# Two graph layers on one core: logits of both array halves one unit ahead, and the order of sums, values and projections at the end of attention

## The chip, the core and the metric

The kernel runs on one core of a Trainium2 chip. The metric is device time in microseconds (us), the median of three runs. One execution was also profiled; where a text speaks of a moment ("763.26") it is microseconds from the start of that execution's span. Engines are named as the profile names them: PE is TensorE's matmuls and PEld its weight loads, DVE is VectorE, ACT ScalarE, POOL GpSimd, SP SyncE. L503 is line 503 of the kernel.

## The reference

`x` is (8, 2048, 256) in float32, `adj` a (2048, 2048) matrix of 0 and 1. Two layers, each with a residual. Layer 0 is attention with 4 heads of 64, masked by `adj`; the softmax is taken separately in each of 8 chunks of 256 keys, and the chunks' contexts are summed. Layer 1 is a graph attention with one head.

```python
h = relu(layernorm(x))
q, k, v = heads(h @ Wq.T + bq), heads(h @ Wk.T + bk), heads(h @ Wv.T + bv)
scores = clip(einsum('bhnd,bhjcd->bhnjc', q, chunks(k)) / 8, -10, 10)
scores = where(mask == 0, -10, scores)
attn = softmax(scores, axis=-1)                    # within one chunk j
ctx = einsum('bhnjc,bhjcd->bhnd', attn, chunks(v)) # sums over chunks too
x = x + layernorm(ctx @ Wo.T + bo + h) * gamma + beta

h = relu(layernorm(x)) @ W
e = leaky_relu((h @ a1)[:, :, None] + (h @ a2)[:, None, :], 0.01)
x = x + relu(softmax(where(adj == 0, -1e9, e)) @ h)
```

(The `h` that is added before the layernorm of layer 0 is the layer's normalised input.)

## The kernel before

The 8 batches run one after the other. Attention of a batch is cut into 32 steps: 4 blocks of 512 queries by 8 chunks of 256 keys. Behind it layer 1 of the batch runs in 16 pieces (`products`, L994), and near its end the next batch's attention starts.

**Tiles of the array.** Heads are 64 wide, so attention uses the 128 x 128 array in tiles of 64 rows by 32 columns: four column tiles side by side, and two halves by rows. Half 0 holds rows 0 to 63, half 1 rows 64 to 127. Both halves can run at once, each on its own data. In a step there is:

- `logits` (L503), four units `o` = 0 to 3. `ORDER = [(0, 1), (0, 0), (1, 1), (1, 0)]` gives the head pair `p` and the half `i` of each, so units 0 and 2 run in half 1 and units 1 and 3 in half 0. A unit fills a PSUM tile `ps_s` of two banks; there are two such tiles.
- `clip` (L543, DVE) takes a unit out of PSUM into `e`, applying the bounds and the mask; `exponentials` (L552, ACT) works in place; `add` (L558, POOL) adds the two 128-key tiles of a head pair into `both`, of which there are two buffers, one per head pair of a step.
- `values` (L519): 32 matmuls. The context lies in two banks `ps_n`, one for each half `c` of the head columns. The "first values" are those with (half, c) = (0, 1) and (1, 0); the "later values" are the other pairing and add to the same banks, now from the other half.
- `sums` (L531): the denominators, 4 matmuls with ones in half 1 and 4 in half 0, into one bank `ps_t`.
- `invert` (L563 and L564, ACT: logarithm and exponential of its negative), `scale` (L573, DVE, two per step), which frees the `ps_n` banks, and `gather` (L578, POOL), which adds the product to the context by a DMA.

A float32 matmul shows as two records in the trace, so a group of one half's logits of a unit is x16, and of both halves x32.

**Fences.** Two halves that write one bank must not run together. `fence(before, after)` (L475) issues a SyncE nop that waits for the matmuls of `before`, and the matmuls of `after` wait for the nop. SyncE also issues many of the DMAs, in the same queue: among them, at the end of attention, the fetches of `hT` for layer 1 (`low.fetch1`) and for the next batch (`ahead.fetch(1)`), and in batch 0 also the stores of `ahead.send(3)`.

**Order.** All engines follow the order in which the program emits. Attention is a software pipeline of frames f = 2 to 34, each with `begin(f)` and `end(f)`, and with pieces of other work (output projection, layernorm, the next batch's work) hung in at 2f and 2f + 1. In a plain frame TensorE does, in this order: later values of step f−3; logits 1 (half 0) and 2 (half 1) of step f−1; first values of step f−2; logits 3 of step f−1 in half 0 around the upper sums of step f−2 in half 1; logits 0 of step f in half 1 around the lower sums of step f−2 in half 0. So half 1 is one logit unit ahead of half 0. Step 0 and the first part of step 1 are computed by `early(0)` to `early(3)` inside the last layer-1 pieces of the batch before.

At the end, frame 32 still has logits 3 of step 31 in half 0, with half 1 without work beside it; frame 33 has the projection q of the next batch's first block (L447), first values of step 31, the projection k, and then `last_sums`: sums and later values of step 31 together. Behind this comes the part between the layers: four token tiles of `low.values` (L843), each followed by `low.keep` with a copy on ACT (L851) and the copy `sd` on DVE (L852); `mid.stats1` (L356 and L357); the values projection `ahead.values` (L461); a part of q (L447); and the output projection (L721). The fourth block's output chain (L757 to L792, DVE, ACT and POOL) runs around it. In the last batch there is no next one: layer 1's `zero.values` take the place of q, and weights of layer 1 (L971, L977) that of k.

Of the kernel before, what the change touches and what calls it, by code (L numbers as in the profile page):

```python
# [28 lines left out]
def gnn_two_layers(  # L29
# [26 lines left out]
    TB = NB // P  # L56
    NNB = N // NB
    NCH = N // CHUNK
    KT = CHUNK // P
# [14 lines left out]
    def ps_t():  # L74
        return ps.tile([P, 512], F32, tag="t", name="ps_t")
# [397 lines left out]
    def fence(before, after):  # L473

        nop = nc.sync.nop()  # L475
        for x in before:
            tc.add_manual_dep(nop.ins, x.ins.name, SYNC, reason="both write one bank of PSUM")
        for x in after:
            tc.add_manual_dep(x.ins, nop.ins.name, SYNC, reason="both write one bank of PSUM")


    class Attention:
# [42 lines left out]

        def sums(self, n, half):
            rows = slice(half * DH, (half + 1) * DH)
            if half:
                self.total[n] = ps_t()
            return [  # L530
                nc.tensor.matmul(  # L531
                    self.total[n][h * Q:(h + 1) * Q, :], ones[rows, :], self.both[n, h // 2][rows, h % 2, :],
                    start=half == 1, stop=half == 0,
                )
                for h in range(HEADS)
            ]
# [46 lines left out]
        def early(self, part):  # L583

            if part == 0:
                for kt in range(KT):
                    self.logits(0, 0, kt)
                    self.logits(0, 1, kt)
            elif part == 1:
                for o in range(2):  # L590
                    self.clip(0, o)
                    self.exponentials(0, o)
                for kt in range(KT):
                    self.logits(0, 2, kt)
                    self.logits(0, 3, kt)
            elif part == 2:
                self.clip(0, 2)
                self.exponentials(0, 2)
                self.clip(0, 3)
                self.add(0, 0)  # L600
            if part == 3:
                for kt in range(KT):
                    self.logits(1, 0, kt)

# [3 lines left out]
        def begin(self, f, pieces=()):  # L610

            self.run(pieces, "first")
            if (f - 3, 0) in self.before:
                made = {}
                for kt in range(KT):
                    for half, c in ((0, 0), (1, 1)):
                        made.setdefault(c, []).extend(self.values(f - 3, half, c, kt))
                for c in range(2):
                    fence(self.before.pop((f - 3, c)), made[c])
            if (f - 1, 0) in self.s:  # L620
                self.clip(f - 1, 0)
            if self.has(f - 3):
                self.invert(f - 3)
            if self.has(f - 2):
                self.exponentials(f - 2, 3)
            if self.has(f - 1):
                self.exponentials(f - 1, 0)
            if self.has(f - 3) and not self.has(f - 1):
                self.scale(f - 3, 0)
                self.scale(f - 3, 1)  # L630
            self.run(pieces, "pe")
            if self.has(f - 1):
                for kt in range(KT):
                    self.logits(f - 1, 1, kt)
                    self.logits(f - 1, 2, kt)
                if self.has(f - 3):
                    self.scale(f - 3, 0)
                    self.scale(f - 3, 1)
            if self.has(f - 2):
                self.add(f - 2, 1)  # L640
            if self.has(f - 3):
                self.gather(f - 3)
            self.rest = pieces

        def end(self, f, pieces=()):
            self.run(pieces, "first")
            if self.has(f - 1):
                self.clip(f - 1, 1)
            self.run(pieces, "pe1")
            if self.has(f - 1):  # L650
                self.clip(f - 1, 2)
            self.run(pieces, "after")
            self.run(self.rest, None)
            if self.has(f - 1):
                self.exponentials(f - 1, 1)
                self.exponentials(f - 1, 2)
            if self.has(f - 2):
                made = {}
                for kt in range(KT):
                    for half, c in ((0, 1), (1, 0)):  # L660
                        made.setdefault(c, []).extend(self.values(f - 2, half, c, kt))
                for c in range(2):
                    self.before[f - 2, c] = made[c]
            if self.has(f - 1):
                self.logits(f - 1, 3, 0)
            if self.has(f - 2) and self.has(f - 1):
                sums = self.sums(f - 2, 1)
            if self.has(f - 1):
                self.logits(f - 1, 3, 1)
            if self.has(f):  # L670
                self.logits(f, 0, 0)
            self.run(pieces, None)
            self.run(pieces, "pe")
            if self.has(f - 2) and self.has(f - 1):
                fence(sums, self.sums(f - 2, 0))
            elif self.has(f - 2):
                self.last_sums(f - 2)
            if self.has(f):
                self.logits(f, 0, 1)
            if self.has(f - 1):  # L680
                self.clip(f - 1, 3)
                self.add(f - 1, 0)

        def last_sums(self, n):

            upper = self.sums(n, 1)
            made = {0: self.values(n, 0, 0, 0), 1: self.values(n, 1, 1, 0)}
            made[0] += self.values(n, 0, 0, 1)
            lower = self.sums(n, 0)
            made[1] += self.values(n, 1, 1, 1)  # L690
            for c in range(2):
                fence(self.before.pop((n, c)), made[c])
            fence(upper, lower)

        @staticmethod
        def run(pieces, kind):
# [5 lines left out]
    class Between:  # L702
        def __init__(self, nb, proj, attention, sd, sums):
            self.nb, self.proj, self.attention, self.sd, self.sums = nb, proj, attention, sd, sums
            self.hn0, self.pp, self.hns = {}, {}, []

            self.adder = nc.gpsimd
# [201 lines left out]
    class Layer1:  # L909
        def __init__(self, b, blocks, sd, sums):  # L910
            self.b, self.blocks, self.sd, self.sums = b, blocks, sd, sums
            self.src = {}
            self.cd = small.tile([P, 2, NT], F32, tag="cd", name="cd", bufs=2)
# [253 lines left out]
    for b in range(B):  # L1167
        sd = small.tile([P, 2, NT], F32, tag="sd", name="sd", bufs=2)
        sums = small.tile([P, NNB, FC], F32, tag="sums", name="sums", bufs=2)
        blocks = [Between(nb, projs[b], att, sd, sums) for nb in range(NNB)]  # L1170
        zero, low, mid, last = blocks
# [24 lines left out]
        if b == 0:  # L1196
# [4 lines left out]
            for nb, ns in enumerate(beats):  # L1201
# [3 lines left out]
                n = ns[-1]  # L1205
# [53 lines left out]
            block.adder = nc.vector  # L1259
        if ahead:  # L1260
            for t in range(TB):
                mid.stats1([t])
                low.values(t, ps_h if t < 2 else ps_t)
                low.keep(t)
            low.sum1()
            zero.fetch1()
            mid.power1()
# [60 lines left out]
        else:  # L1328
# [6 lines left out]
            mid.shift1()  # L1335
            accs[0] = one.accumulators(0)
            early(0)
            mid.norm1(0)
            mid.norm1(1)
# [20 lines left out]
            for t2 in range(2):  # L1360
                last.gamma(t2)
                last.add(t2)
            early(1)
            last.stats1(range(TB))
            last.power1()
            last.shift1()
            weights(3)
            last.norm1(0)
            last.norm1(1)
            early(2)  # L1370
            last.ends(0)
            one.total()
# [90 lines left out]
```

## Time and profile before

| | |
|---|---|
| median of 3 runs | 3513.77 us (3513.32 to 3514.57) |
| the profiled execution | 3513.01 us |
| its span | 3511.2 us, granted TensorE clock 1.000 |
| TensorE matmul, weight load | 3498.5 us, 2300.0 us busy |
| VectorE, ScalarE, GpSimd | 2630.4, 1959.2, 1825.5 us busy |
| one step's matmuls for logits, values, sums | 1335.2, 1121.2, 548.7 us busy in all (L503, L519, L531) |
| first values of step 30 to q, second batch | 763.26 to 769.38 |
| q, first values of step 31, k, `last_sums` | from 769.38, 773.01, 774.88, 778.51 |
| first matmul of layer 1's values (L843), second batch | 781.25 |

Busy times of a row in the profile add up what overlaps only once, so that a TensorE row with one half at work counts as one with both. A row of a timeline joins like instructions that follow each other: start, time from the first start to the last end, engine, line, operation, tile, and how many; in brackets the idle time before it and what ended it.

### The profile page before, as it was taken

The page shows a single profiled execution, that of the slowest core. Times are in us where ns is not written, and L with a number is a line of the kernel's source. Part 1 is how long each engine was busy: PE and PEld are TensorE (multiplying, and loading weights), DVE is VectorE, ACT ScalarE, POOL GpSimd, SP SyncE. Part 2 cuts the span into 40 slices and gives each one's busy share as a digit, 9 for nine tenths or more (in the row PEclk, how much of TensorE's full clock was granted, in tenths as well). Part 3 has the DMA queues.
Part 4 walks back from the last instruction along what each step waited for, and adds up shares of the span by engine and source line. Part 5 has one row for each costly group of instructions (what it writes and reads, how often), then busy time and mean ns, then how long its engine had stood idle before and what let it go on. Part 6 is the DMA issues. An engine that isn't in the chain of part 4 may idle for free.

```text
span 3511.2 us, 104599 instructions
## 1 busy us (share of the span) xinstructions
PE 3498.5 (100%) x46076; PEld 2300.0 (66%) x46076; DVE 2630.4 (75%) x3983; ACT 1959.2 (56%) x2961; POOL 1825.5 (52%) x1198
## 2 busy tenths in 40 slices
PE   9999999999999999999999999999999999999999
PEld 5455775667765577566876758656686655864568
DVE  7887677877678676786767867678686785857876
ACT  6777426763267633676336763367623776147751
POOL 5687017870278702786037850378503784047841
PEclk9999999999999999999999999999999999999999
DMA  7545323443234431444324443244432335224331
GB/s 246 129 108 123 94 87 73 97 113 102 68 87 86 118 100 61 92 93 109 102 61 92 92 105 102 66 91 87 119 105 64 79 85 125 63 55 92 80 78 53
DMA packets 171320, 332.13 MB, mean 95 GB/s; under 512 B 28656, under 2 KB 90352, under 8 KB 170864
## 3 DMA queue, kind: packets, MB, share of 16 engines
q1 hardware_dynamic: 129712, 205.36, 18.6%
q0 software_dynamic: 32832, 119.03, 18.5%
q8 instruction: 360, 5.90, 0.7%
q10 hardware_dynamic: 8320, 1.05, 0.2%
q14 instruction: 96, 0.79, 0.1%
HBM read 156.50 MB, written 51.44 MB: 59 GB/s over the span
## 4 chain that ended last, share of the span: by engine, by line
PE 97%; DVE 1%; ACT 1%; POOL 1%; issue 0%; DMA 0%; ACTq 0%; DVEq 0%; POOLq 0%
PE ps_s L503 25%; PE ps_n L519 25%; PE ps_s L994 12%; PE ps_t L531 6%; PE ps_n L994 6%; PE ps_t L994 6%; PE ps_t L743 2%; PE ps_t L447 2%; PE ps_n L447 2%; PE ps_s L447 2%; PE ps_t L461 2%; PE ps_n L461 1%; PE ps_n L843 1%; PE ps_t L843 1%; PE ps_z L296 0%
## 5 line engine op out<-in xcount | busy, mean ns | idle before, releaser
L543 DVE SCALAR_TENSOR_TENSOR e<-ps_s,bound 128x1024 f32<-128x1024 f32 x1024 | 1219.3, 1221 | 401.3 <-PE ps_s L503 396.4
L558 POOL TENSOR_TENSOR both<-e 128x1024 f32<-128x1024 f32 x512 | 1222.4, 2418 | 541.8 <-PE ps_t L531 244.6
L503 PE MATMUL ps_s<-q,k 64*32 64x512 f32 x16384 | 1335.2, 590 | 0.1
L552 ACT ACTIVATE e<-e 128x1024 f32<-128x1024 f32 x1024 | 1049.3, 1049 | 456.2 <-DVE e L543 438.8
L519 PE MATMUL ps_n<-e,v 64*32 64x512 f32 x16384 | 1121.2, 589 | 0.0
L503 PEld LDWEIGHTS ps_s<-q,k 64*32 64x32 f32 x16384 | 505.2, 106 | 403.3 <-issue 277.9
L519 PEld LDWEIGHTS ps_n<-e,v 64*32 64x32 f32 x16384 | 522.0, 107 | 366.3 <-issue 266.5
L531 PE MATMUL ps_t<-both,ones 64*32 64x512 f32 x4096 | 548.7, 590 | 0.0
L994 PE MATMUL ps_s<-g,w 128*128 128x257 f32 x2048 | 448.5, 380 | 0.0
L994 PEld LDWEIGHTS ps_s<-g,w 128*128 128x128 f32 x2048 | 388.4, 190 | 56.0
L573 DVE TENSOR_TENSOR prod<-ps_n,rz 128x512 f32<-128x512 f32 x448 | 288.7, 687 | 135.0 <-ACT rz L564 86.5
L1017 POOL TENSOR_TENSOR x<-x,r 128x256 f32<-128x256 f32 x124 | 90.7, 745 | 457.8 <-ACT r L1015 457.0
L977 DVE SCALAR_TENSOR_TENSOR w<-bound,w 128x1024 f32<-128x1024 int8 x256 | 314.7, 1229 | 8.7
L367 POOL TENSOR_TENSOR krn<-krn,mv 128x4 f32<-128x4 f32 x28 | 6.8, 243 | 566.1 <-DVE w L971 566.1
L994 PE MATMUL ps_n<-g,w 128*128 128x257 f32 x1024 | 292.4, 382 | 0.0
L994 PE MATMUL ps_t<-g,w 128*128 128x257 f32 x1024 | 289.7, 380 | 0.0
L563 ACT ACTIVATE rz<-ps_t 128x512 f32<-128x512 f32 x256 | 152.6, 596 | 237.3 <-PE ps_t L531 164.2
L971 DVE TENSOR_SCALAR w<-src,cd 128x512 f32<-128x512 f32 x512 | 263.2, 556 | 18.1 <-ACT src L951 14.2
L994 PEld LDWEIGHTS ps_n<-g,w 128*128 128x128 f32 x1024 | 192.8, 190 | 44.3 <-issue 17.6
L578 POOL DMA_DIRECT2D ctxT<-prod x224 | 192.3, 858 | 56.5 <-DVE prod L573 49.5
L531 PEld LDWEIGHTS ps_t<-both,ones 64*32 64x32 f32 x4096 | 152.3, 105 | 100.7 <-SPq L475 45.1
L994 PEld LDWEIGHTS ps_t<-g,w 128*128 128x128 f32 x1024 | 193.8, 189 | 28.2
(139 smaller groups left out, 2975.2 us busy)
## 6 DMA issues: line engine op xcount, KB each, us to landing
ctxT<-prod POOLq DMA_DIRECT2D x224, 512.0 KB, 5.0
bound<-bound_d SPq DMA_DIRECT2D x125, 512.0 KB, 4.7
turned_d<-squares SPq DMA_DIRECT2D x232, 128.0 KB, 2.9
hT<-turned_d SPq DMA_DIRECT2D x58, 512.0 KB, 4.5
rows<-in_adj_dram SPq DMA_DIRECT2D x32, 512.0 KB, 5.3
x<-in_x_dram SPq DMA_DIRECT2D x32, 512.0 KB, 6.3
out_dram<-x SPq DMA_DIRECT2D x31, 512.0 KB, 2.6
xp<-in_x_dram SPq DMA_DIRECT2D x28, 512.0 KB, 4.4
```

The lines of the kernel that those rows point to most:

```text
L447: nc.tensor.matmul(in_key_order(pp) if i == 0 else pp, w[:, di, do * P:(do + 1) * P], h, start=di == 0, stop=di == FC - 1,)
L503: nc.tensor.matmul(self.s[n, o][c * Q:(c + 1) * Q, kt, :], self.k[p][rows, at:at + Q], self.q[p][rows, nb * NB:(nb + 1) * NB], start=True, ...
L519: made.append(nc.tensor.matmul(self.num[n, c][h * Q:(h + 1) * Q, :], self.v[rows, j * KT + kt, at:at + Q], self.e[n, p][rows, i * KT + kt, :],
L531: nc.tensor.matmul(self.total[n][h * Q:(h + 1) * Q, :], ones[rows, :], self.both[n, h // 2][rows, h % 2, :], start=half == 1, stop=half == 0,)
L543: nc.vector.scalar_tensor_tensor(self.e[n, p][:, i * KT:(i + 1) * KT, :], self.s.pop((n, o)), -CLIP * SC, bounds[nb, j // 4][:, j % 4 * KT ...
L552: nc.scalar.activation(e, e, AF.Exp, scale=1.0 / SC)
L558: nc.gpsimd.tensor_tensor(self.both[n, p], e[:, 0], e[:, 1], op=ALU.add)
L573: nc.vector.tensor_tensor(dst[:, c, :], self.num.pop((n, c)), self.rz[n], op=ALU.mult)
L578: nc.gpsimd.dma_start(self.ctxT[nb], self.prod.pop(n), accum_op=ALU.add)
L971: nc.vector.tensor_scalar(w[:, i, :], self.src[nb], self.cd[:, 0, j:j + 1], self.cd[:, 1, j:j + 1], op0=ALU.mult, op1=ALU.max,)
L977: nc.vector.scalar_tensor_tensor(two, bounds1[nb, j // 8][:, j % 8 - 1:j % 8 + 1, :], 0.0, two, op0=ALU.is_gt, op1=ALU.mult)
L994: nc.tensor.matmul(accs[t][:, 0:F + 1], w[:, i, t * P:(t + 1) * P], g[:, j, :], start=j == 0, stop=j == NT - 1,)
```

## The change

Logit unit 1 of the next step moves ahead: in `end(f)` logits 1 and 0 of step f now stand where logits 3 of step f−1 and 0 of step f stood, and in `begin(f)` units 3 and 2 of step f−1 go together. Clips and exponentials follow their units. Later values are emitted with half 1 first. `early(3)` computes units 1 and 0 of step 1 together. Frame 32 has no logits left: it has first values of step 30, lower sums, later values of the same step, upper sums. In frame 33 the upper sums of step 31 come directly behind q, then first values and lower sums; the inversion is emitted ahead of k, and later values come behind k. `sums` no longer depends on which half is first. Between the layers, the values of a token tile and their copies are emitted ahead of the statistics of the tile before.

```diff
         def sums(self, n, half):
             rows = slice(half * DH, (half + 1) * DH)
-            if half:
+            first = n not in self.total
+            if first:
                 self.total[n] = ps_t()
...
-                    start=half == 1, stop=half == 0,
+                    start=first, stop=not first,
...
             if part == 3:
                 for kt in range(KT):
+                    self.logits(1, 1, kt)
                     self.logits(1, 0, kt)
+                self.clip(1, 1)
...
         def begin(self, f, pieces=()):
...
             if (f - 3, 0) in self.before:
-                made = {}
-                for kt in range(KT):
-                    for half, c in ((0, 0), (1, 1)):
-                        made.setdefault(c, []).extend(self.values(f - 3, half, c, kt))
-                for c in range(2):
-                    fence(self.before.pop((f - 3, c)), made[c])
+                self.later_values(f - 3)
             if (f - 1, 0) in self.s:
                 self.clip(f - 1, 0)
-            if self.has(f - 3):
+            if (f - 3) in self.total:
                 self.invert(f - 3)
-            if self.has(f - 2):
-                self.exponentials(f - 2, 3)
             if self.has(f - 1):
+                self.exponentials(f - 1, 1)
                 self.exponentials(f - 1, 0)
-            if self.has(f - 3) and not self.has(f - 1):
+            if self.has(f - 3) and not self.has(f):
                 self.scale(f - 3, 0)
                 self.scale(f - 3, 1)
             self.run(pieces, "pe")
             if self.has(f - 1):
                 for kt in range(KT):
-                    self.logits(f - 1, 1, kt)
+                    self.logits(f - 1, 3, kt)
                     self.logits(f - 1, 2, kt)
-                if self.has(f - 3):
+                if self.has(f) and self.has(f - 3):
                     self.scale(f - 3, 0)
                     self.scale(f - 3, 1)
...
         def end(self, f, pieces=()):
...
-                self.clip(f - 1, 1)
+                self.clip(f - 1, 3)
...
-                self.exponentials(f - 1, 1)
+                self.exponentials(f - 1, 3)
                 self.exponentials(f - 1, 2)
...
-                self.logits(f - 1, 3, 0)
...
-                sums = self.sums(f - 2, 1)
...
-                self.logits(f - 1, 3, 1)
...
+            if self.has(f):
+                self.first_values(f - 2)
+                self.logits(f, 1, 0)
+                sums = self.sums(f - 2, 1)
+                self.logits(f, 1, 1)
+                self.logits(f, 0, 0)
+                self.run(pieces, None)
+                self.run(pieces, "pe")
+                fence(sums, self.sums(f - 2, 0))
+                self.logits(f, 0, 1)
+                self.clip(f, 1)
+            elif self.has(f - 1):
+                self.first_values(f - 2)
+                sums = self.sums(f - 2, 0)
+                self.later_values(f - 2)
+                fence(sums, self.sums(f - 2, 1))
+                self.run(pieces, None)
+                self.run(pieces, "pe")
+            elif self.has(f - 2):
+                sums = self.sums(f - 2, 1)
+                self.first_values(f - 2)
+                fence(sums, self.sums(f - 2, 0))
+                self.run(pieces, None)
+                self.invert(f - 2)
+                self.run(pieces, "pe")
+                self.later_values(f - 2)
...
-        def last_sums(self, n):
...
+        def later_values(self, n):
+            made = {0: [], 1: []}
+            for kt in range(KT):
+                for half, c in ((1, 1), (0, 0)):
+                    made[c] += self.values(n, half, c, kt)
             for c in range(2):
                 fence(self.before.pop((n, c)), made[c])
...
             for t in range(TB):
-                mid.stats1([t])
                 low.values(t, ps_h if t < 2 else ps_t)
                 low.keep(t)
+                if t:
+                    mid.stats1([t - 1])
+            mid.stats1([TB - 1])
```

In the changed kernel the lines from `sums` on lie one lower (sums L532, clip L544, add L559, scale L574), `fence` stays at L475, and those between the layers lie five lower (L848, L857).

More of the change, by code (lines that the diff above doesn't have):

```diff
@@ L599, in early @@
                 self.clip(0, 3)
+                self.exponentials(0, 3)
                 self.add(0, 0)
@@ L654, in end @@
             if self.has(f - 1):
-                self.exponentials(f - 1, 1)
+                self.exponentials(f - 1, 3)
                 self.exponentials(f - 1, 2)
[L657 to L663, printed above, removed]
-            if self.has(f - 1):
-                self.logits(f - 1, 3, 0)
@@ L666, in end @@
-            if self.has(f - 2) and self.has(f - 1):
-                sums = self.sums(f - 2, 1)
-            if self.has(f - 1):
-                self.logits(f - 1, 3, 1)
[L670 to L679, printed above, removed]
@@ L680, in end @@
-            if self.has(f - 1):
-                self.clip(f - 1, 3)
-                self.add(f - 1, 0)
-        def last_sums(self, n):
[L686 to L690, printed above, removed]
+            if self.has(f):
[24 more added lines that the diff above has]
+                self.later_values(f - 2)
@@ new lines, in end, with first_values @@
+            if self.has(f - 1):
+                self.add(f - 1, 0)
+        def first_values(self, n):
+            made = {0: [], 1: []}
+            for kt in range(KT):
+                for half, c in ((0, 1), (1, 0)):
+                    made[c] += self.values(n, half, c, kt)
+            for c in range(2):
+                self.before[n, c] = made[c]
+        def later_values(self, n):
+            made = {0: [], 1: []}
+            for kt in range(KT):
+                for half, c in ((1, 1), (0, 0)):
+                    made[c] += self.values(n, half, c, kt)
@@ L691, in last_sums @@
             for c in range(2):
                 fence(self.before.pop((n, c)), made[c])
-            fence(upper, lower)
         @staticmethod
```

## The prediction

> **What bounds the kernel now.** I read the page first (engine rows, clock, chain that ended last), then TensorE's timeline inside a batch and across the place where attention of a batch ends and layer 1 begins (I call it the joint), then GpSimd's and VectorE's timelines there, and the list of waits.
>
> ```profile
> PE 3498.5 (100%) x46076; PEld 2300.0 (66%) x46076; DVE 2630.4 (75%) x3983; ACT 1959.2 (56%) x2961; POOL 1825.5 (52%) x1198
> PE 97%; DVE 1%; ACT 1%; POOL 1%; issue 0%; DMA 0%; ACTq 0%; DVEq 0%; POOLq 0%
> ```
>
> PE is busy all the time at granted clock 1.00 and 97% of the chain is its own. Busy does not mean full, though: the array is cut into two halves of 64 rows, and a row of this trace is as busy with one half running as with both. So PE's time has to be counted in passes. A plain frame:
>
> ```profile
> 606.14 2.00 PE L519 MATMUL ps_n<-e,v 64*32 64x512 f32 x32
> 607.86 2.00 PE L503 MATMUL ps_s<-q,k 64*32 64x512 f32 x32
> 609.58 2.00 PE L519 MATMUL ps_n<-e,v 64*32 64x512 f32 x32
> 613.87 2.00 PE L519 MATMUL ps_n<-e,v 64*32 64x512 f32 x32
> ```
>
> x32 with both halves takes 607.86−606.14 = 1.72 us, which is 4 passes of 0.43 (0.429). From one later-values group to the same one a frame on, 613.87−606.14 = 7.73 = 18 passes, and 18 is what each half has to do (8 logits, 8 values, 2 sums). Plain frames are full. Here the Trainium skill ("Trainium Kernel Development and Optimization", section "Best Practices") has a rule: judge the distance to the roofline by the share of weight loads, not of matmuls. Row: PEld 66%. By the rule a third, 0.34 × 3511 = 1190 us, would be open; by the pass count, nothing inside a frame. I take the pass count, so gains can come only from where a half stands idle. Those places:
>
> ```profile
> 925.38 1.95 PE L503 MATMUL ps_s<-q,k 64*32 64x512 f32 x32
> 943.41 1.92 PE L503 MATMUL ps_s<-q,k 64*32 64x512 f32 x16
> 945.26 0.92 PE L994 MATMUL ps_n<-g,w 128*128 128x257 f32 x3
> 763.26 2.23 PE L519 MATMUL ps_n<-e,v 64*32 64x512 f32 x32
> 769.38 3.70 PE L447 MATMUL ps_s<-hT,wqT 128*128 128x512 f32 x8
> 773.01 1.95 PE L519 MATMUL ps_n<-e,v 64*32 64x512 f32 x32
> 774.88 3.70 PE L447 MATMUL ps_s<-hT,wkT 128*128 128x512 f32 x8
> 781.25 2.01 PE L843 MATMUL ps_s<-w1s,hT 128*128 128x258 f32 x8
> 784.84 1.89 PE L461 MATMUL ps_n<-wvT,hT 128*128 128x256 f32 x8
> 787.28 1.99 PE L461 MATMUL ps_t<-wvT,hT 128*128 128x256 f32 x8 [0.55 <-DVE sd L852]
> ```
>
> At 943.41 a lone x16 takes 1.85 us, as long as an x32 (1.88). From the first values of step 30 (763.26) to q (769.38) are 6.12 us = 14 passes, of which half 1 needs 10.
>
> **The change, part by part** (clock of the second batch).
>
> *Early units and frame 32.* Logits (1,1) join (1,0) at 943.41: x32 for x16, +0.03. In frame 32 the four passes of logit unit 3 of step 31 are gone from half 0, and later values of step 30 move in from frame 33. What remains after the first values is 6 passes per half. But half 1's later values now stand directly behind half 0's first values in the same PSUM bank, and a fence (a SyncE nop) orders them. Row: `PEld ps_t L531 <- SPq L475`, 45.1 us in 247 waits, 0.18 each, where four passes lie between the parties. Here none do: half 0's last record starts 764.89, lasts 0.59, the nop and the reload bring half 1 to about 765.68 in place of 765.08. The skill's "TensorEngine Tiling (Array Packing)", section "Gotcha 1: PSUM Pressure", speaks against the new order: two row tiles may not use one bank at a time and software must synchronise. Priced by the row this is 0.2, by the two parties back to back 0.6; I take 0.6 (0.4 per batch apart, 3 us in all). Then 6 × 0.429 + 0.11: q at 768.36. Gain 1.02.
>
> *Frame 33, last sums ahead of k.* Sums of step 31 in half 1 now come directly behind q. They need `both` of step 31, two GpSimd adds:
>
> ```profile
> 767.90 4.68 POOL L558 TENSOR_TENSOR both<-e 128x1024 f32<-128x1024 f32 x2 [0.83 <-PE ps_t L531]
> ```
>
> There are two such buffers, so those adds wait for the sums of step 30. These end at 768.43 now (half 1 is last). So: 768.43 + 0.17 + 4.68 = 773.28, + 0.09 to PE = 773.37. q ends 768.36 + 3.63 = 771.99. A new wait of 1.4 us, with first values of step 31, lower sums, k and all of layer 1 queued behind it. Before, q, V and k (9.1 us) lay between and covered it. Then sums/values/sums 2.69, k 3.63, later values 1.88: L843 at 781.57, before 781.25. Net +0.32: the wait takes back the gain of frame 32. Bounds of the wait: 0 if PE or the adds run 1.4 apart from this sum, 2 if GpSimd's adds are slowed by the fetches beside them.
>
> *Copies ahead of statistics; invert ahead of k's copies.*
>
> ```profile
> PE ps_t L461 <- DVE sd L852: 4.3, 7, 1.0
> PEld ps_t L461 <- DVE sd L852: 7.1, 7, 1.4
> 782.75 1.29 DVE L573 TENSOR_TENSOR prod<-ps_n,rz 128x512 f32<-128x512 f32 x2 [11.89 <-ACT rz L564]
> 786.54 0.43 DVE L356 BATCH_NORM_STATS2 stats<-x 128x6 f32<-128x256 f32 x1 [1.31 <-POOL x L792]
> ```
>
> The third values group of L461 waits for the third sd copy, which stands behind statistics that wait for GpSimd's L792, which stands behind scale and gather of the last step. With copies first and the inversion 5 us earlier that goes: 787.28−784.84 = 2.44 against 1.83 for the next such group, so −0.6, and −0.1 for the refill: −0.7 in 7 batches. The moved statistics are wanted only by the norm, after two output groups (3.5 us).
>
> *SyncE's queue.* The last fence nop now waits for sums at about 774.6, and the fetches of hT for layer 1 and the next block stand behind it: issued 8 us later than the 766.71 and 767.14 of before. First parts landed 4.9 us after issue: 779.6, wanted by L843 at 781.57. Hidden with 2 us to spare in batches 1 to 6, by the upper sums' wait itself. In batch 0 four stores (3.5 us) stand between, the second fetch waits for the last one's landing (page: 2.9), and the nops of later values are behind it: about +1.7 there.
>
> *Plain frames.* `scale` of column half 0 now waits for both halves of later values, since half 1 is emitted first. Path: last matmul 0.589 + 0.12 + two scales 1.29 + 0.09 = 2.09, against 5 passes = 2.145 until half 1's first values write the bank: slack 0.05, no loss. Exponentials and adds get some 2 us more room, but nothing waits long for them (`PEld ps_t L531 <- POOL both L558`: 2.6 us in all). Frames in which VectorE has other work (statistics, z) lose the slack: some 10 us of such work per batch, put at +0.1 per batch, and +1 to +2 in batch 0 with its 32 z finds. Bounds −1 (added room) to +4; I take +2.
>
> *Last batch.* No `ahead`: the same wait of 1.4 stands behind the layer-1 products' values, and the scale of the last step comes behind weights on VectorE: +0.5 to +1.1, taken 0.8.
>
> **Sum** against the profiled execution (span 3511.2, 1.8 around it, 3513.01): an ordinary batch +0.03 +0.32 −0.7 = −0.4, six of them −2.4; batch 0 −0.4 +1.7 = +1.3; last +0.8; frames +2. Total about +1.7: 3514.7. The median of the runs is 3513.77, 0.76 above the profiled execution, so 3515.4. Measurement of this kernel can tell some 0.2%, 7 us, from no change.
>
> **The rivals.**
>
> *A, slower: scale behind both halves.* For it: the slack is 0.05 us by the sum above, while the halves lie 0.1 to 0.3 apart from frame to frame. Place: VectorE's L574 in every plain frame; point of decision: a half 0 ending over 0.05 us after half 1's turn. If it decides, and PE takes up 0.05 per frame, 28 × 8 frames cost 11: 3526; at 0.1 twice that. Against it: only half 1 is held, and once held it stays behind; then the path has its slack again.
>
> *B, faster: no wait for GpSimd behind q.* If the adds of step 31 start after half 0's sums, or run beside other work more quickly, the 1.4 go: 8 × −1.4 = −11: 3504. For it: before, the same adds began 0.83 us after an idle, so they are early enough to move. Against: the built program has the adds wait for the sums of half 1 of step 30.
>
> *C, later fetch.* If the fetch takes 8 us (two fetches and a gather share the queues) and not 4.9, L843 waits 1.1 us in seven batches: +8: 3523.
>
> *D, the change does not do what it says.* The built order of TensorE shows it does: pairs at the early units, no logits in frame 32.
>
> **How the numbers follow.** Base case 0.47, centre 3515, own range 3508 to 3521 by the bounds of the wait (±0.6 × 8) and of the frames. A 0.2 with some of C (0.1): above 3521. B 0.23: below 3507. Range 3503 to 3527 leaves the ends of A and B out. Faster 0.23, same 0.46, slower 0.31.
>
> **What would show it.** Right: 64 fewer half-idle passes, x32 at every early unit; q 1.0 us sooner after the first values of step 30; a wait of L532 on L559 of about 1.4 in eight places; the wait of L461 on sd gone; plain frames still 7.72; fetches issued 8 us later without a wait of L843 on them outside batch 0. Wrong: plain frames of 7.77 or longer with L519 held by L574 (A); no wait of L532 in frame 33 (B); L843 waiting for a DMA (C).

## The result: 5.1 us slower, and where the time lies

The changed kernel takes 3518.95 us (3518.3 to 3520.78, 22 runs), the kernel before 3513.81 beside it: a ratio of 1.0015, 95% interval 1.0009 to 1.0021. (One of the 22 executions of the kernel before took 20027.53 us and stands apart; the others lie between 3513.24 and 3515.13.) The interval leaves out 1, so the loss is small but real: 0.15%, inside the 0.2% put down as "no change", and 3.6 us above the forecast of 3515.4. The profiled execution of the changed kernel took 3519.78 us, its span is 3518.0; the span of before was 3511.2. So the traces to be compared differ by 6.8 us.

Cutting both traces at the first sums of each batch and at those of step 29, that is at the last plain frame, gives a ledger in us. The first line is the time ahead of the first sums; "joint and layer 1" is the rest of a batch, up to the first sums of the next:

| stretch | before | after | difference |
|---|---|---|---|
| setup, up to the first sums | 77.25 | 78.28 | +1.0 |
| batch 0: frames; joint and layer 1 | 247.09; 198.55 | 248.75; 199.14 | +1.7; +0.6 |
| batches 1 to 6, mean of one: frames | 234.65 | 235.37 | +0.72 |
| batches 1 to 6, mean of one: joint and layer 1 | 198.38 | 197.94 | −0.44 |
| batch 7: frames; joint and layer 1 | 235.28; 154.91 | 235.72; 156.27 | +0.4; +1.4 |

1.0 + 1.7 + 0.6 + 6 × 0.72 − 6 × 0.44 + 0.4 + 1.4 = 6.8. The first line can't be put down to the change: across all nine profiled kernels the first sums lay between 77.25 and 79.67, and a kernel whose setup is that of before had 77.97. What is left is a small gain at the joint and a loss in the frames.

The profile's first rows show neither. PE is as busy as it was, and its share of the chain went from 97% to 96%:

```profile
PE 3501.4 (100%) x46076; PEld 2347.9 (67%) x46076; DVE 2619.4 (74%) x3983; ACT 1960.8 (56%) x2961; POOL 1815.6 (52%) x1191
PE 96%; DVE 1%; POOL 1%; ACT 1%; DMA 1%; issue 1%; SPq 0%; POOLq 0%; DVEq 0%; ACTq 0%
```

**The joint of the second batch, after.** Timeline of TensorE (start, time, line, operation, count, idle before):

```profile
767.22 2.30 PE L519 MATMUL ps_n<-e,v 64*32 64x512 f32 x31
769.71 2.11 PE L519 MATMUL ps_n<-e,v 64*32 64x512 f32 x32
772.41 3.70 PE L447 MATMUL ps_s<-hT,wqT 128*128 128x512 f32 x8
776.04 1.05 PE L532 MATMUL ps_t<-both,ones 64*32 64x512 f32 x4
777.38 0.62 PE L532 MATMUL ps_t<-both,ones 64*32 64x512 f32 x2 [0.29 <-POOL both L559]
780.11 3.70 PE L447 MATMUL ps_s<-hT,wkT 128*128 128x512 f32 x8
783.74 1.95 PE L519 MATMUL ps_n<-e,v 64*32 64x512 f32 x32
785.62 2.01 PE L848 MATMUL ps_s<-w1s,hT 128*128 128x258 f32 x8
789.21 1.89 PE L461 MATMUL ps_n<-wvT,hT 128*128 128x256 f32 x8
790.93 1.89 PE L461 MATMUL ps_t<-wvT,hT 128*128 128x256 f32 x8
```

First values of step 30 to q: 772.41−767.22 = 5.19, before 6.12. Behind q the upper sums of two heads start at once (776.04), those of the other two only at 777.38. The bracket says 0.29 us, because the first two heads count as busy until 777.09; what PE lost is the whole 1.34 from 776.04. What it waited for is the second of the two adds in this row:

```profile
772.65 4.67 POOL L559 TENSOR_TENSOR both<-e 128x1024 f32<-128x1024 f32 x2 [1.57 <-PE ps_t L532]
```

772.65 + 4.67 = 777.32, 0.06 ahead of the matmul. From q to layer 1's first matmul are 785.62−772.41 = 13.21, before 11.87. And from there on the two L461 groups follow each other without a gap: 1.72 apart, before 2.44.

**A plain frame.** The sums of three consecutive frames, before (L531) and after (L532):

```profile
709.16 0.61 PE L531 MATMUL ps_t<-both,ones 64*32 64x512 f32 x4
716.89 0.61 PE L531 MATMUL ps_t<-both,ones 64*32 64x512 f32 x4
724.61 0.61 PE L531 MATMUL ps_t<-both,ones 64*32 64x512 f32 x4
```

```profile
711.67 0.61 PE L532 MATMUL ps_t<-both,ones 64*32 64x512 f32 x4
719.42 0.61 PE L532 MATMUL ps_t<-both,ones 64*32 64x512 f32 x4
727.18 0.61 PE L532 MATMUL ps_t<-both,ones 64*32 64x512 f32 x4
```

Before 7.73 and 7.72, after 7.75 and 7.76. No wait in PE's list names it. The list of weight loads does name the scale, but it names it less often after (`PEld ps_n L519 <- DVE prod L574: 16.2, 66, 0.5`) than before (37.8 us in 164 waits), where the waits were covered. The loss appears in VectorE's timeline, where the scale of a step stands behind the later values of that step (first row before, second row after):

```profile
712.04 1.29 DVE L573 TENSOR_TENSOR prod<-ps_n,rz 128x512 f32<-128x512 f32 x2 [0.17 <-PE ps_n L519]
```

```profile
716.34 1.29 DVE L574 TENSOR_TENSOR prod<-ps_n,rz 128x512 f32<-128x512 f32 x2 [0.61 <-PE ps_n L519]
```

The single records say how much later. Take the start of the last matmul of later values, in whichever half. Over all 256 steps the first scale begins 0.41 us (median) behind it in the kernel before, and 0.78 behind it in the changed kernel. Both scales together then take 1.29, and the weight loads of half 1's first values, which wait for the second scale, start 0.05 later. In the frame before the one shown the first scale begins at 708.59; half 1's weight loads start at 709.932 and its matmuls at 709.937, just when that half is free. In the frame of the kernel before that is shown, half 1's weights came 0.29 us ahead of their matmuls (713.382 and 713.668). With only 0.005 ahead, matmuls of this pass last 0.61 in place of 0.59, and the next pass starts 14 to 44 ns late. Of the 240 steps 0 to 29 of all batches, 202 show such longer matmuls behind the second scale in the changed kernel, with weights 0.004 us ahead (median); before, 2 do.

The same frame shows why the order of emission matters. Half 0 is emitted second, but it runs ahead all the same (the halves are told apart by the lower sums, which run in half 0 just before): the last matmul of its later values ends at 708.11 by the records, half 1's at 708.40. The semaphore that the scale of half 0's bank waits for rises only at 708.51, behind both.

**Waits of PE** in the changed kernel (waited for: us in total, times, longest), the ones that before did not have (those of the setup and those of 0.2 are left out):

```profile
PE ps_t L532 <- POOL both L559: 2.0, 7, 0.3
PE ps_t L848 <- DMA hT<-turned_d: 1.4, 1, 1.4
PE ps_n L519 <- SPq L475: 1.3, 1, 1.3
PE ps_s L848 <- DVE sd L857: 0.9, 1, 0.9
PE ps_t L532 <- SPq L475: 0.7, 1, 0.7
```

Seven times the wait behind q; once, at the joint of batch 0, later values behind the fence; in batch 7 the values of layer 1 behind an sd copy and behind the fetch; and once, in a frame of batch 0, lower sums behind their fence. `PE ps_t L461 <- DVE sd L852` is gone.

### The profile page after: what moved, and what is told of

The parts are those of the page before. It is cut to its first block, busy times and chain, and to the rows that moved or that the text cites. A ratio compares the mean times of both kernels' runs of the same rounds, so it can differ in the third digit from the quotient of the medians.

```text
span 3518.0 us, 104607 instructions
## 1 busy us (share of the span) xinstructions
PE 3501.4 (100%) x46076; PEld 2347.9 (67%) x46076; DVE 2619.4 (74%) x3983; ACT 1960.8 (56%) x2961; POOL 1815.6 (52%) x1191
## 4 chain that ended last, share of the span: by engine, by line
PE 96%; DVE 1%; POOL 1%; ACT 1%; DMA 1%; issue 1%; SPq 0%; POOLq 0%; DVEq 0%; ACTq 0%
PE ps_s L503 25%; PE ps_n L519 25%; PE ps_s L999 12%; PE ps_n L999 6%; PE ps_t L532 6%; PE ps_t L999 6%; PE ps_t L748 2%; PE ps_n L447 2%; PE ps_t L447 2%; PE ps_n L461 2%; PE ps_t L461 1%; PE ps_t L848 1%; PE ps_n L848 1%; PE ps_s L447 1%; POOL both L559 1%
## 5 line engine op out<-in xcount | busy, mean ns | idle before, releaser
L559 POOL TENSOR_TENSOR both<-e 128x1024 f32<-128x1024 f32 x512 | 1220.6, 2415 | 553.6 <-PE ps_t L532 409.8
L544 DVE SCALAR_TENSOR_TENSOR e<-ps_s,bound 128x1024 f32<-128x1024 f32 x1024 | 1208.9, 1219 | 328.6 <-PE ps_s L503 270.9
L503 PE MATMUL ps_s<-q,k 64*32 64x512 f32 x16384 | 1365.1, 590 | 0.4
L519 PE MATMUL ps_n<-e,v 64*32 64x512 f32 x16384 | 1164.6, 590 | 1.3 <-SPq L475 1.3
L503 PEld LDWEIGHTS ps_s<-q,k 64*32 64x32 f32 x16384 | 569.6, 106 | 379.6 <-issue 180.7
L519 PEld LDWEIGHTS ps_n<-e,v 64*32 64x32 f32 x16384 | 533.1, 106 | 346.8 <-issue 135.4
L532 PE MATMUL ps_t<-both,ones 64*32 64x512 f32 x4096 | 561.3, 590 | 2.6 <-POOL both L559 2.0
L574 DVE TENSOR_TENSOR prod<-ps_n,rz 128x512 f32<-128x512 f32 x448 | 288.5, 686 | 217.7 <-issue 118.8
L532 PEld LDWEIGHTS ps_t<-both,ones 64*32 64x32 f32 x4096 | 152.3, 105 | 95.1 <-SPq L475 40.2
```

Of the source, the lines that this page charges most:

```text
L503: nc.tensor.matmul(self.s[n, o][c * Q:(c + 1) * Q, kt, :], self.k[p][rows, at:at + Q], self.q[p][rows, nb * NB:(nb + 1) * NB], start=True, ...
L519: made.append(nc.tensor.matmul(self.num[n, c][h * Q:(h + 1) * Q, :], self.v[rows, j * KT + kt, at:at + Q], self.e[n, p][rows, i * KT + kt, :],
L532: nc.tensor.matmul(self.total[n][h * Q:(h + 1) * Q, :], ones[rows, :], self.both[n, h // 2][rows, h % 2, :], start=first, stop=not first,)
L544: nc.vector.scalar_tensor_tensor(self.e[n, p][:, i * KT:(i + 1) * KT, :], self.s.pop((n, o)), -CLIP * SC, bounds[nb, j // 4][:, j % 4 * KT ...
L559: nc.gpsimd.tensor_tensor(self.both[n, p], e[:, 0], e[:, 1], op=ALU.add)
L574: nc.vector.tensor_tensor(dst[:, c, :], self.num.pop((n, c)), self.rz[n], op=ALU.mult)
```

## The experiments

Seven kernels, each against the kernel before. Theory T: the frames lose because the first scale waits for both halves. Theory J: the joint gains in frame 32 and in the copies, and gives it back in the wait for GpSimd's adds.

**Later values half 0 first** (changed kernel, one line):

```diff
         def later_values(self, n):
-                for half, c in ((1, 1), (0, 0)):
+                for half, c in ((0, 0), (1, 1)):
```

> The changed kernel with the later values emitted half 0 first, as before the change; nothing else. Theory T (scale behind both halves): the scale of column half 0 waits for half 0 alone again, starts some 0.3 us earlier, half 1's first values find their bank free in time, and plain frames go from 7.75 back to 7.72. About 25 plain frames in 8 batches, 0.027 each: 5.4 us, so about 3513.5 against 3518.95. Rival R1 (what costs is that the halves change their order of issue twice a frame, not the scale): this edit removes that too, so the same 3513.5; the run with the scales swapped tells the two apart. Rival R2 (the new pairing of logit units 1 and 0 shifts the column tiles against each other, and that costs): 7.75 stays, 3519.

Measured 3514.48 us, ratio to before 1.0002 (0.9994 to 1.0011): 4.5 below the changed kernel. Its frames of batches 1 to 6 take 234.78 a batch (235.37 in the changed kernel) and its joints as long as there (197.94). Consecutive sums are 7.72 apart:

```profile
709.66 0.61 PE L532 MATMUL ps_t<-both,ones 64*32 64x512 f32 x4
717.38 0.61 PE L532 MATMUL ps_t<-both,ones 64*32 64x512 f32 x4
725.11 0.61 PE L532 MATMUL ps_t<-both,ones 64*32 64x512 f32 x4
```

The first scale is back at 0.40 after the last matmul. The pairing of logit units 1 and 0 stayed and costs nothing in these frames, so R2 is out; R1 (the changed order of issue) and T are both still there.

**Scale of column half 1 first** (changed kernel; the order of the matmuls untouched; the same swap at the end of attention and the place where the product's tile is taken are left out):

```diff
...
-                self.scale(f - 3, 0)
                 self.scale(f - 3, 1)
+                self.scale(f - 3, 0)
```

> The changed kernel with the two scales of a step swapped: column half 1 first, then column half 0. The order of the matmuls stays as changed. Theory T: the first scale now waits only for half 1, whose matmuls are emitted first; the second needs both, but has 0.65 us until its turn. The first starts about 0.07 us earlier than the 0.78 us after the last later value of the changed kernel, which is more than the 0.02 to 0.04 that each frame loses: frames of 7.72 to 7.73, about 3514. Rival R1 (order of issue): 7.75 stays, about 3519.

Measured 3515.6 us, ratio 1.0005 (0.9997 to 1.0013): 3.4 below the changed kernel. Its slowest execution, 3517.02, lies below the changed kernel's fastest, 3518.3. Frames of 234.86 a batch, and sums 7.73 and 7.72 apart:

```profile
711.98 0.73 PE L532 MATMUL ps_t<-both,ones 64*32 64x512 f32 x4
719.71 0.73 PE L532 MATMUL ps_t<-both,ones 64*32 64x512 f32 x4
727.43 0.73 PE L532 MATMUL ps_t<-both,ones 64*32 64x512 f32 x4
```

The first scale begins 0.71 after the last matmul where it was 0.78: 0.07 sooner, and that was enough. In one of these frames half 1's weights come 0.035 us ahead (708.809 and 708.844), and the matmuls last 0.59. The halves change their order of issue as they do in the changed kernel, so R1 is out. T holds: a path on VectorE that ends 0.02 to 0.04 too late.

**K ahead of the sums** (changed kernel; frame 33 as before, with `last_sums` as it was there):

```diff
             elif self.has(f - 2):
-                sums = self.sums(f - 2, 1)
                 self.first_values(f - 2)
-                fence(sums, self.sums(f - 2, 0))
                 self.run(pieces, None)
-                self.invert(f - 2)
                 self.run(pieces, "pe")
-                self.later_values(f - 2)
+                self.last_sums(f - 2)
+                self.invert(f - 2)
```

> The changed kernel with frame 33 as before the change: q, first values, k, then sums and later values of step 31 together, inversion last; frame 32, the pairs and the copies ahead of statistics stay as changed. Theory J (the sums directly behind q wait 1.34 us for GpSimd's adds and give back the gain of frame 32; the fence ahead of the fetches is what the first and last batch pay): no wait of the sums on the adds, the stretch from q to L848 goes from 13.2 to 11.9 us, no wait on the late fetch in batches 0 and 7. 8 times 1.3, less some 0.2 per batch for the later inversion: -8 to -10, about 3510. Rival I (the early inversion is what took the stall off L461): the stall of about 0.7 comes back in 7 batches, and only -4 to -5 remain, about 3514.

Measured 3507.48 us, ratio 0.9981 (0.9974 to 0.9988): 11.5 below the changed kernel, and below the kernel before. TensorE at its joint (nine lines were added, so layer 1's values are L857 here):

```profile
770.49 3.70 PE L447 MATMUL ps_s<-hT,wqT 128*128 128x512 f32 x8
774.12 1.95 PE L519 MATMUL ps_n<-e,v 64*32 64x512 f32 x32
776.00 3.70 PE L447 MATMUL ps_s<-hT,wkT 128*128 128x512 f32 x8
779.63 0.63 PE L532 MATMUL ps_t<-both,ones 64*32 64x512 f32 x4
782.37 2.01 PE L857 MATMUL ps_s<-w1s,hT 128*128 128x258 f32 x8
785.96 1.89 PE L461 MATMUL ps_n<-wvT,hT 128*128 128x256 f32 x8
787.69 1.89 PE L461 MATMUL ps_t<-wvT,hT 128*128 128x256 f32 x8
```

```profile
770.73 4.67 POOL L559 TENSOR_TENSOR both<-e 128x1024 f32<-128x1024 f32 x2 [1.60 <-PE ps_t L532]
```

q to layer 1: 782.37−770.49 = 11.88, against 13.21. The sums start with no gap; the adds end at 775.40, before k has even begun. The L461 groups are 1.73 apart: the stall did not come back though the inversion is late again. So the copies removed it, not the early inversion; rival I is out. Per batch the joint takes 196.58 (197.94 in the changed kernel): −1.36, the wait of 1.34. The wait of batch 0 on the fence and that of batch 7 on the fetch are gone with it; the 0.9 on an sd copy stays.

**Sums amid the later values** (changed kernel, frame 32 only; the new lines stand in a method of their own, and the fences of the later values are left out):

```diff
                 self.first_values(f - 2)
-                sums = self.sums(f - 2, 0)
-                self.later_values(f - 2)
-                fence(sums, self.sums(f - 2, 1))
+                upper = self.sums(f - 2, 1)
+                made = {0: self.values(f - 2, 0, 0, 0)}
+                lower = self.sums(f - 2, 0)
+                made[1] = self.values(f - 2, 1, 1, 0)
+                made[0] += self.values(f - 2, 0, 0, 1)
+                made[1] += self.values(f - 2, 1, 1, 1)
...
+                fence(upper, lower)
```

> The changed kernel with another order in frame 32: behind the first values come the upper sums in half 1 and the later values of half 0 with the lower sums between their two key tiles, then the later values of half 1. Both sums of step 30 are then done two passes (0.86 us) earlier. Theory J: the adds of step 31 start 0.86 earlier, and since the sums behind q wait for the adds, k and all behind it come 0.86 sooner: 8 times, -7, about 3512; the wait on L559 falls from 1.3 to about 0.5, or stays 1.1 if q comes sooner as well. Rival: the adds are held by something else (exponentials of step 31 or GpSimd's own queue), and nothing moves: 3519.

Measured 3512.15 us, ratio 0.9996 (0.9988 to 1.0004): 6.8 below the changed kernel, as theory J has it. Joint 196.99 a batch (−0.95). GpSimd's adds begin 0.67 after it fell idle, where it was 1.57:

```profile
772.00 4.68 POOL L559 TENSOR_TENSOR both<-e 128x1024 f32<-128x1024 f32 x2 [0.67 <-PE ps_t L532]
776.28 1.07 PE L532 MATMUL ps_t<-both,ones 64*32 64x512 f32 x6
```

The adds set the time of the sums behind q: moved 0.9 earlier, everything behind them moved as much.

**Copies first only** (kernel before, this part alone):

```diff
             for t in range(TB):
-                mid.stats1([t])
                 low.values(t, ps_h if t < 2 else ps_t)
                 low.keep(t)
+                if t:
+                    mid.stats1([t - 1])
+            mid.stats1([TB - 1])
```

> The kernel before with one part of the change: between the layers, values and copies of a token tile ahead of the statistics of the tile before. Theory: the third values group of L461 no longer waits for its sd copy behind statistics that wait for GpSimd; 0.6 us of idle PE and 0.1 of refill go in 7 batches: -4 to -5, about 3509. Rival: the copies still stand behind the scale of the last step, which here comes later than in the changed kernel (inversion behind k's copies), so that a part of the stall stays: -1 to -3, about 3512.

Measured 3507.7 us, ratio 0.9981 (0.9974 to 0.9988): 6.2 below the kernel before, more than either expected. The joint is shorter by 0.82 in each of batches 1 to 6:

```profile
784.64 1.89 PE L461 MATMUL ps_n<-wvT,hT 128*128 128x256 f32 x8
786.37 1.89 PE L461 MATMUL ps_t<-wvT,hT 128*128 128x256 f32 x8
788.10 1.88 PE L447 MATMUL ps_n<-hT,wqT 128*128 128x512 f32 x4
```

L461 takes 1.73 twice; before it took 2.44 and 1.83. 0.71 + 0.10 = 0.81. Six times 0.82 are 4.9; the rest came in batch 0, whose joint fell from 198.55 to 197.30.

**Fetches ahead of the fence** (changed kernel):

```diff
             elif self.has(f - 2):
+                self.run(pieces, None)
                 sums = self.sums(f - 2, 1)
                 self.first_values(f - 2)
                 fence(sums, self.sums(f - 2, 0))
-                self.run(pieces, None)
```

> The changed kernel with the SyncE pieces of frame 33 (fetches of hT, in the first batch stores as well) emitted ahead of the fence of the last sums; nothing else. Theory S (the fence holds the queue up): the wait of L848 on the fetch in the last batch (1.4 us) and that of later values on the fence in the first (1.3 us) go: -2.5 to -3, about 3516. In batches 1 to 6 nothing changes, since the fetch lands in time there. Rival: the transfer itself is late, whatever its place in the queue: 3519.

Measured 3517.7 us, ratio 1.0011 (1.0005 to 1.0018): 1.25 below the changed kernel, half of what was expected. The intervals of the two ratios overlap, so the times alone don't show this gain; the traces do. The joint of batch 0 is 1.0 shorter, and its wait of 1.3 is gone. Batch 7 did not gain: the wait on the fetch went and another took its place, that of a values group on the scale of the last step, which stands behind layer 1's weights on VectorE:

```profile
3380.61 2.01 PE L848 MATMUL ps_t<-w1s,hT 128*128 128x258 f32 x8
3383.87 2.01 PE L848 MATMUL ps_n<-w1s,hT 128*128 128x258 f32 x8 [1.25 <-DVE prod L574]
```

**Half 0 first and k ahead**, both edits above together:

> Two edits together that each made the changed kernel faster: later values emitted half 0 first, and frame 33 with k ahead of the sums, as before the change. Theories T and J concern different places (plain frames, the joint), so the gains add: -4.5 and -11.5 on 3518.95, about 3503, 0.3% below the kernel before. If they share a cause (the scale that is late also holds the joint): 3505 to 3507.

Measured 3503.26 us (7 runs), ratio 0.997 (0.9959 to 0.9982), 10.7 below the kernel before and 15.7 below the changed one. The two gains add (4.5 + 11.5 = 16.0): two causes in two places. Against the copies alone (3507.7), what remains of the change, frame 32 and the pairs, is worth 4.4: its joint takes 196.61 a batch against 197.56, −0.95, less what the frames lose in a few places (234.78 against 234.64).

## Why the prediction came out as it did

It said "same", and 0.15% is that, within its own range of 3508 to 3521. The mechanism it built, a gain in frame 32 that the wait for the adds takes back, is what the traces show. Three of its signs failed: plain frames of 7.75 in place of 7.72, no wait for the adds in batch 7, and a wait of L848 on the fetch there. Its steps, one by one, for batches 1 to 6 unless said otherwise:

- **Frame 32, gain 1.02.** Measured 6.12−5.19 = 0.93. The fence cost less than the 0.6 put down: half 1's first values start their last pass at 768.92, so it is free at 769.35, and its later values begin at 769.71: 0.36, between the two prices weighed. But half 1 also came 0.3 to 0.4 behind half 0 out of the frame before, and the two together make the sum right; that they cancel is luck. By the records the hold was not even for half 0, whose first values end at 769.24: two nops stand in a row, and the first (769.59) waits for half 1's own first values, which end at 769.53. No run here puts both halves on one bank at once, so the rule on banks that the prediction cites is not tested; what shows is the price of keeping it.
- **Frame 33, a wait of 1.4, q to L843 13.21.** Measured 1.34 and 13.21. Rival B, no wait, fell: the buffer of `both`, freed by the last sums of step 30, is what starts the adds.
- **Copies ahead, −0.7.** Measured −0.82, by the run of that part alone. What the prediction credited in addition, the inversion 5 us earlier, does nothing for this stall.
- **Joint in all, −0.4 per batch.** Measured −0.44.
- **SyncE's queue.** Hidden in batches 1 to 6 as said: the fetch is issued at 778.68, 11.46 behind the first values of step 30; before it was 766.71, 3.45 behind them. That is 8.0 later, and L848 does not wait. In batch 0 the predicted +1.7 was 1.0, by the run that moves the fetches.
- **Last batch, 0.8.** Measured +1.4 at its joint. The wait for the adds, on which the 0.8 rested, does not show there; in its place stand 0.9 on an sd copy and 1.4 on the fetch. The prediction had the scale behind the weights, but left out that the late fetch has less cover here. Fetch and scale lie side by side, so that taking one wait away brings out the other.
- **Plain frames: the step that failed in size.** "Slack 0.05, no loss" was summed as 0.589 + 0.12 + 1.29 + 0.09 = 2.09 against 2.145. The first two terms, 0.71 from the start of the last matmul to the scale, measure 0.78 in the changed kernel; that makes 2.16 and no slack. The 0.71 was measured where the scale waits for one half; here its semaphore rises behind both. What the path needed was also a little more than the bank being free in time: weights that come in with no lead cost a few hundredths even where the matmul starts on time. This is rival A, at its place, with 0.02 to 0.03 a frame in place of 0.05. What decides is another half than the prediction named: it is half 1 that ends last, not half 0. So what was held against it, that half 1 once held gives the path its slack back, did not come true: the path begins with half 1's own last matmul, and a later half 1 takes the scale along. Frames cost 1.7 + 6 × 0.72 + 0.4 = 6.4 in all, of which the run with half 0 first takes 5.0 back by the same ledger; the sum had 2. These 4.4 are most of the 5.1 by which the traces differ more than forecast (6.8 against 1.7); the setup's 1.0 and the last batch's 0.6 add to them, and batch 0's joint, 0.7 under its forecast, takes off.
- **Passes or weight loads.** The prediction set the pass count against the rule on weight loads and named only one of the two measures of that section: the Trainium skill ("Trainium Kernel Development and Optimization", section "Best Practices") has MFU, the share of peak arithmetic, beside it. The count fits the runs: PEld is 66% busy before and 67% after, no kernel here has plain frames under 7.72, and the best gains 10.7 us, not 1190.

Batch 0's frames are still 0.8 us longer than before with the later values half 0 first (247.89 against 247.09). Most of that lies in one frame, 8.61 against 7.99, and it is not VectorE's: the lower sums wait for their fence nop, which stands in SyncE's queue behind a DMA whose issue took 1.26 us, and 0.36 before. The two rows in the run with half 0 first:

```profile
283.98 0.63 PE L532 MATMUL ps_t<-both,ones 64*32 64x512 f32 x4 [0.65 <-SPq L475]
282.61 1.26 SPq L178 DMA_DIRECT2D bound<-bound_d  x1
```

Two points stay open: why that issue took longer, and whether a third buffer for `both` would take the wait behind q away at its root, which was not tried.

## What to carry to other kernels

When work is pulled out of a place where it stood idle-looking, ask what it covered: k between q and the last sums was the cover of two adds on GpSimd and of a fetch on SyncE's queue, and frame 32's gain went straight into the wait. In a loop that is full to the last pass, the order of two groups that run side by side still decides whom a semaphore waits for; a scale that waits for the second group in place of the first cost 0.02 to 0.03 us a frame and 5 us in all. A change of several parts is worth running part by part: one of these parts alone (copies first) gave 6 us, and its sum with the others hid it.

## What the runs showed of the hardware

- Matmuls whose weights came in only 5 ns ahead lasted 0.61 in place of 0.59 us, and the next pass of their half began 14 to 44 ns late (202 of 240 frames of the changed kernel, 2 before). In a frame with 35 ns ahead they lasted 0.59. PE's list of waits shows none of this: by its records nothing was idle.
- Of two groups that run side by side in the two halves, the one emitted second ended first, but its semaphore rose only behind the other's end: half 0 ended at 707.14 and half 1 at 707.36 in the run with the scales swapped, and the semaphore rose at 707.385 for half 1 and at 707.478 for half 0. So a scale that waits for the first of the two began 0.71 us after the last start (median), one that waits for the second 0.78.
- The rows of a half-full array hide a wait: 1.34 us of lost time behind q is listed as 0.29, since two of the four column tiles counted as busy.
